# Where the weight pieces and the next pair's first chunks stand among the slots of a recurrent and feed-forward kernel

## The chip, the cores and the metric

The kernel runs on one core of one Trainium2 chip. The metric is device time in microseconds (us). Several runs are shown for a kernel and their median is what is compared; one further execution was taken by the hardware profiler, and every duration, wait and window in this document comes from that one.

## The reference

The input x holds 8 sequences of 512 tokens with 512 features. It is normalised, run through a bidirectional stack of four minimal gated recurrent layers, fused, added back, then run through a feed-forward layer with ternary weights and added back again. Cut to what matters:

```python
z = sigmoid(h @ Wz.T + bz)
h_tilde = tanh(h @ Wz.T + bz)            # the same weights serve z and h_tilde, and both directions
a = clip(1 - z, 1e-8, 1 - 1e-8)
h_new = linear_scan(a, z * h_tilde)      # along the tokens; backwards for the second direction
h = layernorm(h_new + (h if layer > 0 else 0))
...
x = x + concat(h_fwd, h_bwd) @ fusion_W.T + fusion_b
gamma = mean(abs(W)) + 1e-6              # for W_fc (2048 x 512) and W_proj (512 x 2048)
Wq = sign(W) * minimum(round(abs(W / gamma)), 1)
x = x + layernorm(gelu(layernorm(x) @ Wq_fc.T)) @ Wq_proj.T
```

The mean of all absolute values of a weight matrix must be known before any of its entries can be made ternary, and the ternary weights are needed only by the feed-forward part.

## The kernel before, in words

Everything runs on tiles of 128 partitions by 512 fp32 elements. A sequence has four feature **chunks** of 128 features (in the recurrent part, tokens along the free axis) and four token tiles (in the fusion and the normalisations). The work has two parts: a recurrent part over four **pairs** of sequences (the loop `for b in range(0, B, 2)` at L677), and a feed-forward part (L880 and below) that this change leaves alone.

**One chunk of a layer** is `gates` (L409): four matmuls into a PSUM tile u (L414), three activations on ScalarE that make a, t and z (`factors`, L428), then on VectorE a clip (L437), a product (L438), a scan (L442) and, in layers 1 and 2, the residual sum (L497). In the last layer the residual sums stand apart (`sums`, L503). A **state** is a sequence and a direction; a pair has four, and the order of a pair is layers 1, 2, 3, in each layer the four states, in each state the four chunks. Layer 0 has both directions in one chunk (`first_layer`, L444): four matmuls (L457), a scaling on VectorE (L464), the activations, clip, product and two scans, forwards and backwards. The eight layer-0 chunks of the next pair (`firsts`) are spread over the end of the present one.

**Normalising** a state turns its chunks into token tiles by transposes through the identity (`turned`, L293, into one of two PSUM tiles pt), takes statistics on VectorE (`stats`, L149 to L160, the power on GpSimd at L156), normalises on ScalarE (L166, L167) and turns the result back (`back`, transposes L302, activation L308). After the last layer only the statistics are taken (`norm_last`).

**Fusion** (`fusion`, L513) makes one token tile from eight matmuls over two PSUM tiles pu (L528), adds a bias (L523) and two scaled terms on VectorE (L536), and stores the tile to DRAM from SP's queue (L539). A pair has eight such tiles.

**The order is written out by hand**, per engine, as a sequence of **slots** (`slot`, L391). A slot issues, in this order: its own matmuls, the due scalings of layer-0 chunks, at most one or two shares of normalisation work for earlier states, the due clips and scans of layer-0 chunks, its own clip, product and scan (for fusion, the two scaled terms), the due residual sums, and the ScalarE ends of the shares. [...]

**The weight pieces** are a list `extra` that `slot` serves at its end (L401 to L406). There are 32 pieces of 128 by 512 for each of two passes. An `absolute` piece loads a part of a weight matrix from SP's queue (`staged`, L548, three buffers) and sums its absolute values on ScalarE (L557). `total` and `threshold` (L560, L565) then make the limits, with one small matmul that waits for a VectorE reduction. A `quantised` piece loads the part again, makes it ternary with two VectorE instructions (`ternary`, L171 and L172) and stores it to DRAM from SP's queue (L583, two buffers). Each time a piece is served, the loads of the next two are issued too. The list is filled with the 32 absolute pieces and the four small steps at the first pair, and with the 32 quantised pieces at the second (L679 to L690). The slot counter decides when one is served: every second slot in the first pair, every fourth from the second pair on (`pace`). So they fall in whatever the slot holds, layers or fusion alike.

**The next pair's layer-0 chunks:** two of the eight stand in the last state's last layer (before its chunks 1 and 3, the argument `between` of `layer`, L490), and one behind each of the first six fusion tiles (L722 to L726).

Of the kernel before, what the change touches and what calls it, by code (L numbers as in the profile page):

```python
# [24 lines left out]
def kernel(  # L25
# [28 lines left out]
    L = gru_wT.shape[0]  # L54
# [147 lines left out]
    NW = NQ * NC_  # L202
# [4 lines left out]
    with rec:  # L207
# [7 lines left out]
        now = [0]  # L215
# [20 lines left out]
        def shares(cap):  # L236


            last = []
            for q in (turns, backs):  # L240
                some = []
                for i in range(2):
                    if not q or not ready(q[0][0]):
                        break
                    at, piece = q[0][:2]
                    late = (at.at if isinstance(at, Tokens) else at) + piece < now[0]
                    if i >= cap and not late:
                        break
                    some.append(take(q))
                last = some + last  # L250
            return last
# [14 lines left out]
        def need(*keys):  # L266

            while any(left.get(k) for k in keys):
                slot(None, 2)
# [108 lines left out]
        def x_shares():  # L378
            return [take(q) for q in (xturns, xbacks) if q and ready(q[0][0])]

        pace = [2]
        extra = []

        stages = []
# [1 line left out]
        def due(kind):  # L386
            for s in [s for s in stages if s[0] <= now[0] and s[1] == kind]:
                stages.remove(s)
                s[2]()

        def slot(work=None, cap=1):  # L391
            end = work() if work is not None else None
            due("factors")
            last = shares(cap) + x_shares()
            due("scans")
            if end is not None:
                end()
            due("resid")
            for f in last:
                f()  # L400
            if extra and now[0] % pace[0] == 0:  # L401
                for piece in extra[:3]:
                    if piece[0] is not None:
                        piece[0]()
                        piece[0] = None
                extra.pop(0)[1]()  # L406
            now[0] += 1

        def gates(h, l, o, name, scans):  # L409

            def work():
                u = ps_u.tile([P, S], F32, tag="u", name=f"u_{name}")
                for c in range(NC_):
                    nc.tensor.matmul(  # L414
                        u, lhsT=gw[l][:, c, ts(o, P)], rhs=h[:, c, :],
                        start=(c == 0), stop=(c == NC_ - 1),
                    )
                z = zp.tile([P, S], F32, tag="z", name=f"z_{name}")
                zlive[0] += 1
                a, t = factors(u, z, l, o, name)  # L420

                def end():
                    product(a, z, t)
                    scans(a, z)
                return end
            return work
# [53 lines left out]
                return work  # L480
            return [chunk(o) for o in range(NC_)]

        def layer(s, l, between=()):
            while s not in state:
                slot(None, 2)
            need(s)
            zs = []
            h = state[s]
            for o in range(NC_):
                if between and o % 2:  # L490
                    slot(between.pop(0))

                def scans(a, z, o=o):
                    scan(z, a, z, s[1] == 1)
                    zs.append(z)
                    if l < L - 1:
                        nc.vector.tensor_tensor(z, z, h[:, o, :], ALU.add)  # L497
                    elif o == NC_ - 1:

                        for c in range(NC_):  # L500
                            def sums(c=c):
                                zlive[0] -= 1
                                nc.vector.tensor_tensor(h[:, c, :], zs[c], h[:, c, :], ALU.add)  # L503
                            stages.append((now[0] + c, "resid", sums))
                slot(gates(h, l, o, f"{s[0]}{s[1]}_{l}_{o}", scans))
            now[0] -= 1
            if l < L - 1:
                norm(s, zs, f"{s[0]}{s[1]}_{l}", 2)
            else:
                norm_last(s, f"{s[0]}{s[1]}_{l}")  # L510
            now[0] += 1
# [53 lines left out]
        def threshold(name, tot):  # L565

            pth = ps_u.tile([P, 512], F32, tag="u", name=f"pth_{name}")
            nc.tensor.matmul(pth[:, 0:1], lhsT=ones, rhs=tot, start=True, stop=True)
            absmean = const.tile([P, 1], F32, name=f"absmean_{name}")
            nc.vector.tensor_scalar(absmean, pth[:, 0:1], 1.0 / (H * F), Q_EPS, ALU.mult, ALU.add)  # L570
            hi = const.tile([P, 1], F32, name=f"hi_{name}")
            nc.vector.tensor_scalar(hi, absmean, 0.5, None, ALU.mult)
            lo = const.tile([P, 1], F32, name=f"lo_{name}")
            nc.vector.tensor_scalar(lo, absmean, -0.5, None, ALU.mult)
            limits[name] = (hi, lo)

        def quantised(part, i, name):
            w = []

            def go():  # L580
                q = qp.tile([P, 512], F32, tag="q", name=f"{name}q_{i}")
                ternary(q, w[0], limits[name])
                nc.sync.dma_start(out=wq[name][i // NC_][:, i % NC_, :], in_=q)  # L583
            extra.append([lambda: w.append(staged(part, i, f"{name}b")), go])

        def load_fc(i):
            fcq.append(wpool.tile([P, NC_, 512], F32R, tag=f"w{i}", name=f"fcq{i}"))
            nc.sync.dma_start(out=fcq[i].bitcast(F32), in_=wq["fc"][i])
# [74 lines left out]
        for i in range(2):  # L663
            s = const.tile([P, P], F32, name=f"fpick{i}")
# [11 lines left out]
            slot(lambda d=d: fold_sums(d), 2)  # L676
        for b in range(0, B, 2):  # L677
            last_pair = b + 2 == B
            if b == 2:  # L679
                pace[0] = 4  # L680
                for name, part in (("fc", fc_part), ("pw", proj_part)):
                    for i in range(NW):
                        quantised(part, i, name)
            if b == 0:
                for name, part in (("fc", fc_part), ("pw", proj_part)):
                    for i in range(NW):
                        absolute(part, i, name)
                    tots = []
                    extra.append([None, lambda n=name, tots=tots: tots.append(total(n))])
                    extra.append([None, lambda n=name, tots=tots: threshold(n, tots[0])])  # L690
            for l in range(1, L):
                if last_pair:
                    load_fc(l - 1)
                    if l == 1:
                        combined()
                        load_pw(0)
                for s in ((b, 0), (b, 1), (b + 1, 0), (b + 1, 1)):
                    if l == L - 1 and not last_pair and s[1] == 0:
                        norm_x(s[0] + 2, now[0])
                    if l == L - 1 and s[1] == 0:  # L700
                        load_pair("f", s[0])
                    if l == L - 2 and not last_pair and s[1] == 1:
                        load_pair("n", s[0] + 2)
                        load_xT(s[0] + 2)
                    if last_pair and s == (b, 1) and l == L - 2:
                        load_y(0)
                    if last_pair and s == (b, 0) and l == L - 1:
                        norm_y(0)
                    if l == L - 1 and not last_pair and s == (b + 1, 1):


                        firsts = first_layer(b + 2) + first_layer(b + 3)
                        layer(s, l, firsts)
                    else:
                        layer(s, l)
                    if s[0] == 1 and l == 1:
                        slot(lambda d=s[1]: fold(d))
                        if s[1] == 1:
                            slot(fold_bias)
            if last_pair:  # L720
                load_fc(L - 1)
            for i in range(2):  # L722
                for tile_ in fusion(b + i):
                    slot(tile_, 2)
                    if not last_pair and firsts:
                        slot(firsts.pop(0))  # L726
                if last_pair and i == 0:
                    load_pw(1)
                    load_pw(2)
# [18 lines left out]
    for i in range(2):  # L748
        s = const.tile([P, P], F32, name=f"pick{i}")
# [130 lines left out]
    for j in range(B * NF + LAG):  # L880
        b, k = divmod(j, NF)
# [74 lines left out]
```

## Time and profile before

| what | value |
|---|---|
| runs shown, median of 3 | 1767.56 us (1766.42 to 1767.70) |
| the profiled execution, its own time | 1769.31 us |
| its span, first to last instruction | 1767.3 us |
| what lies around the span | 2.0 us |
| mean granted TensorE clock | 0.990 |
| recurrent part in the span | 0 to 1268.3 us |
| feed-forward part | 1268.3 to 1767.3 us |

The recurrent part has stages that can be told apart in the trace by the first matmul of each: the layers by the groups of L414, the fusions by L528. From the start of one to the start of the next:

| pair | layer 1 | layer 2 | layer 3 | fusion, with the next pair's layer 0 |
|---|---|---|---|---|
| 0 | 61.6 to 152.2 | to 222.4 | to 297.7 | to 384.2 |
| 1 | 384.2 to 453.9 | to 523.5 | to 604.0 | to 691.7 |
| 2 | 691.7 to 762.1 | to 831.9 | to 914.4 | to 1002.1 |
| 3 | 1002.1 to 1072.6 | to 1141.5 | to 1208.4 | to 1268.3 (no layer 0) |

The absolute pieces run from 69.3 to 376.7 us, so through the whole first pair; the quantised ones from 436.3 to 1038.7 us, from the second pair's layer 1 into the last pair's layer 1. PE is TensorE's matmuls, PEld its weight loads, DVE is VectorE, ACT ScalarE, POOL GpSimd, SP the engine whose queue issues most DMAs. An fp32 matmul appears as two records.

### The profile page before, as it was taken

What the parts mean: (1) busy time and instruction counts of PE and PEld (TensorE: products, weight loads), DVE (VectorE), ACT (ScalarE), POOL (GpSimd) and SP (SyncE); (2) the same over time, 40 slices, a digit from 0 to 9 for tenths busy, and PEclk for the clock granted to TensorE, in tenths of its full rate; (3) what the DMA queues carried; (4) which work ended last, traced back from release to release, by engine and by line L of the source; (5) the groups of instructions that cost most, each with busy time, mean ns of one, the idle gap of its engine ahead of it and who ended that gap; (6) DMA issues with size and microseconds to landing.
All of it is one profiled execution on the core that took longest, in us unless ns stands there. A gap on an engine that the chain in (4) does not pass through costs nothing.

```text
span 1767.3 us, 19729 instructions
## 1 busy us (share of the span) xinstructions
PE 1721.4 (97%) x6424; PEld 1046.7 (59%) x6424; DVE 1451.1 (82%) x2865; ACT 1066.2 (60%) x1836; POOL 214.5 (12%) x334
## 2 busy tenths in 40 slices
PE   7989999999999999999999999999999999999998
PEld 3554554455554445555444455554588888888886
DVE  6977989779999977999897799997468778778876
ACT  2887884358886325787632588872156556566653
POOL 1111111111111111111111111111000000000000
PEclk9999999999999999999999999999999999999999
DMA  7002210110231111123101201101301101101100
GB/s 262 12 30 78 96 54 19 48 48 13 72 102 54 28 38 54 36 72 107 49 24 42 96 13 48 59 14 42 126 1 48 38 11 48 49 9 40 48 24 24
DMA packets 46454, 91.73 MB, mean 52 GB/s; under 512 B 5264, under 2 KB 5264, under 8 KB 45328
## 3 DMA queue, kind: packets, MB, share of 16 engines
q1 hardware_dynamic: 45488, 88.91, 14.8%
q10 hardware_dynamic: 864, 1.57, 0.3%
q8 instruction: 50, 0.82, 0.2%
q14 instruction: 52, 0.43, 0.1%
HBM read 65.30 MB, written 25.17 MB: 51 GB/s over the span
## 4 chain that ended last, share of the span: by engine, by line
PE 62%; DVE 29%; issue 6%; ACT 2%; POOL 0%; DVEq 0%; DMA 0%; POOLq 0%; ACTq 0%
PE u L414 16%; PE pu L528 12%; PE ph L782 12%; PE po L809 11%; DVE z L442 7%; DVE st L149 5%; DVE z L438 4%; PE u L457 4%; PE pt L293 3%; DVE z L497 2%; PE pf L302 2%; DVE a L437 2%; DVE mv L151 1%; DVE ve L155 1%; DVE st_x L149 1%
## 5 line engine op out<-in xcount | busy, mean ns | idle before, releaser
L414 PE MATMUL u<-xT,gw 128*128 128x512 f32 x768 | 351.1, 601 | 0.0
L414 PE MATMUL u<-h,gw 128*128 128x512 f32 x768 | 350.7, 600 | 0.0
L442 DVE TENSOR_TENSOR_SCAN z<-a,z 128x512 f32<-128x512 f32 x224 | 274.3, 1224 | 7.8
L149 DVE BATCH_NORM_STATS2 st<-pt 128x6 f32<-128x512 f32 x256 | 177.2, 692 | 71.7 <-PE pt L293 71.2
L786 ACT ACTIVATE g<-ph 128x512 f32<-128x512 f32 x128 | 76.4, 597 | 245.9 <-PE ph L782 245.9
L414 PEld LDWEIGHTS u<-xT,gw 128*128 128x128 f32 x768 | 141.2, 194 | 141.0 <-issue 141.0
L414 PEld LDWEIGHTS u<-h,gw 128*128 128x128 f32 x768 | 141.1, 194 | 140.7 <-issue 140.7
L156 POOL TENSOR_TENSOR rs<-ve,mhalf 128x1 f32<-128x1 f32 x192 | 122.9, 640 | 704.1 <-DVE nmu L160 649.1
L809 PE MATMUL po<-pwq,ghi 128*128 128x512 f32 x512 | 203.6, 398 | 0.0
L809 PE MATMUL po<-pwq,glo 128*128 128x512 f32 x512 | 199.9, 390 | 0.0
L782 PE MATMUL ph<-yhi,fcq 128*128 128x512 f32 x512 | 199.8, 390 | 0.0
L782 PE MATMUL ph<-ylo,fcq 128*128 128x512 f32 x512 | 199.7, 390 | 0.0
L431 ACT ACTIVATE a<-u,ngb 128x512 f32<-128x512 f32 x192 | 131.2, 683 | 99.6 <-PE u L414 98.7
L438 DVE TENSOR_TENSOR z<-z,t 128x512 f32<-128x512 f32 x224 | 153.7, 686 | 16.6 <-ACT z L433 16.6
L167 ACT ACTIVATE tok<-pt,nmr,rs 128x512 f32<-128x512 f32 x192 | 149.2, 777 | 6.4
L797 DVE TENSOR_TENSOR acc<-acc,g 128x512 f32<-128x512 f32 x112 | 77.4, 691 | 91.1 <-ACT g L786 90.1
L433 ACT ACTIVATE z<-u,gb 128x512 f32<-128x512 f32 x192 | 132.6, 691 | 0.0
L431 ACT ACTIVATE a<-z,ngb 128x512 f32<-128x512 f32 x32 | 23.1, 722 | 179.7 <-DVE z L464 179.7
L432 ACT ACTIVATE t<-u,gb 128x512 f32<-128x512 f32 x192 | 131.0, 682 | 0.0
L302 PE MATMUL pf<-ident,tok 128*128 128x128 f32 x768 | 116.8, 276 | 13.0 <-ACT tok L167 10.4
L293 PEld LDWEIGHTS pt<-ident,z 128*128 128x128 f32 x640 | 78.8, 142 | 84.6 <-issue 52.4
L166 ACT ACTIVATE nmr<-nmu,rs 128x1 f32<-128x1 f32 x192 | 56.5, 294 | 107.5 <-POOL rs L156 96.8
(138 smaller groups left out, 2711.0 us busy)
## 6 DMA issues: line engine op xcount, KB each, us to landing
xn<-in_x_dram SPq DMA_DIRECT2D x32, 256.0 KB, 4.6
xf<-in_x_dram SPq DMA_DIRECT2D x32, 256.0 KB, 4.3
x<-xf SPq DMA_DIRECT2D x32, 256.0 KB, 2.0
xy<-x SPq DMA_DIRECT2D x32, 256.0 KB, 4.1
out_dram<-xy SPq DMA_DIRECT2D x32, 256.0 KB, 2.0
xT<-in_xt_dram SPq DMA_DIRECT2D x7, 1024.0 KB, 7.0
fca<-in_fc_wT_dram SPq DMA_DIRECT2D x16, 256.0 KB, 2.9
pwa<-in_proj_wT_dram SPq DMA_DIRECT2D x16, 256.0 KB, 2.7
```

The costliest lines, as they stand in the source:

```text
L149: nc.vector.bn_stats(st, src)
L167: nc.scalar.activation(dst, src, AF.Identity, bias=nmr, scale=rs)
L293: nc.tensor.transpose(pt[:, ts(c, P)], zs[c][:, ts(t, P)], ident)
L302: nc.tensor.transpose(pf[:, ts(t, P)], toks[t][:, ts(c, P)], ident)
L414: nc.tensor.matmul(u, lhsT=gw[l][:, c, ts(o, P)], rhs=h[:, c, :], start=(c == 0), stop=(c == NC_ - 1),)
L431: nc.scalar.activation(a, u, AF.Sigmoid, bias=ngb[:, l, o : o + 1], scale=-1.0)
L433: nc.scalar.activation(z, u, AF.Sigmoid, bias=gb[:, l, o : o + 1])
L438: nc.vector.tensor_tensor(z, z, t, ALU.mult)
L442: nc.vector.tensor_tensor_scan(dst[:, d], a[:, d], z[:, d], 0.0, ALU.mult, ALU.add)
L528: nc.tensor.matmul(pu, lhsT=hs[d][:, c, ts(t, P)], rhs=fw[:, d * NC_ + c, :], start=(c == 0), stop=(c == NC_ - 1),)
L782: nc.tensor.matmul(ph, lhsT=w, rhs=ys[b][c][i], start=(c == 0 and i == 0), stop=(c == NC_ - 1 and i == 1),)
L809: nc.tensor.matmul(po[b][t], lhsT=part[:, ts(t, P)], rhs=pwq[k // NP_][:, k % NP_, :], start=(k == 0 and i == 0), stop=(k == NF - 1 and i ...
```

## The change

The pace is gone: a slot no longer serves pieces. A new function `pieces(n)` serves n of them where it is called, and it is called in two places.

In the first pair, inside `layer`: behind every second chunk of layers 1 and 2 and behind every chunk of layer 3, as long as more than 32 entries are left in the list. With 36 entries ahead of the quantised ones and 8, 8 and 16 places, 32 are served there; the last four (two absolute pieces, the second total and threshold) go to the first fusion.

Behind every fusion tile of every pair, one piece behind tiles 0 and 2 of a sequence and two behind tiles 1 and 3. The quantised pieces are put on the list from the start, so eight of them are served in the first pair's fusion and twelve in each of the next two; none is left for the layers.

The two layer-0 chunks leave the last layer. All eight stand behind fusion tiles: two each behind tiles 0 and 2 of the first sequence, one each behind its tiles 1 and 3 and behind tiles 0 and 1 of the second.

```diff
-        pace = [2]
         extra = []
...
+        def pieces(n):
+
+            for _ in range(min(n, len(extra))):
+                for piece in extra[:3]:
+                    if piece[0] is not None:
+                        piece[0]()
+                        piece[0] = None
+                extra.pop(0)[1]()
...
         def slot(work=None, cap=1):
...
-            if extra and now[0] % pace[0] == 0:
-                for piece in extra[:3]:
-                    if piece[0] is not None:
-                        piece[0]()
-                        piece[0] = None
-                extra.pop(0)[1]()
             now[0] += 1
...
-        def layer(s, l, between=()):
+        def layer(s, l):
...
             for o in range(NC_):
-                if between and o % 2:
-                    slot(between.pop(0))
...
                 slot(gates(h, l, o, f"{s[0]}{s[1]}_{l}_{o}", scans))
+
+                if s[0] < 2 and (l == L - 1 or o % 2) and len(extra) > 2 * NW:
+                    pieces(1)
...
-            if b == 2:
-                pace[0] = 4
-                for name, part in (("fc", fc_part), ("pw", proj_part)):
-                    for i in range(NW):
-                        quantised(part, i, name)
             if b == 0:
...
+                for name, part in (("fc", fc_part), ("pw", proj_part)):
+                    for i in range(NW):
+                        quantised(part, i, name)
...
-                    if l == L - 1 and not last_pair and s == (b + 1, 1):
-
-
-                        firsts = first_layer(b + 2) + first_layer(b + 3)
-                        layer(s, l, firsts)
-                    else:
-                        layer(s, l)
+                    layer(s, l)
...
+            firsts = [] if last_pair else first_layer(b + 2) + first_layer(b + 3)
             for i in range(2):
-                for tile_ in fusion(b + i):
+                for t, tile_ in enumerate(fusion(b + i)):
                     slot(tile_, 2)
-                    if not last_pair and firsts:
-                        slot(firsts.pop(0))
+                    pieces(1 + t % 2)
+                    for _ in range(2 if i == 0 and t % 2 == 0 else 1):
+                        if firsts:
+                            slot(firsts.pop(0))
```

## The prediction, on record before the changed kernel was run

> **What bounds the kernel now.** First the page as a whole: TensorE (PE) is busy nearly throughout and most of the final chain is PE's, but a modelled busy share hides short stalls, and almost a third of the chain is VectorE's (DVE).
>
> ```profile
> PE 1721.4 (97%) x6424; PEld 1046.7 (59%) x6424; DVE 1451.1 (82%) x2865; ACT 1066.2 (60%) x1836; POOL 214.5 (12%) x334
> ...
> PE 62%; DVE 29%; issue 6%; ACT 2%; POOL 0%; DVEq 0%; DMA 0%; POOLq 0%; ACTq 0%
> ```
>
> So I read it by stage, in the view of windows (columns: stretch, length, then busy us and instructions of PE, PEld, DVE, ACT, POOL, then clock and DMA): layer 3 and fusion of pair 1, layer 3 of pair 2, layers 2 and 3 of pair 3, and the few us after a stall.
>
> ```profile
> 523.50:604.00 80.50, 75.18 (x251) 38.53 (x250) 74.56 (x151) 44.61 (x75) 13.69 (x22) 0.98 0.17 56
> 604.00:691.70 87.70, 86.65 (x274) 43.30 (x273) 67.58 (x129) 28.07 (x47) 10.41 (x16) 1.00 0.15 45
> 831.90:914.40 82.50, 77.11 (x251) 39.03 (x250) 74.86 (x152) 44.75 (x76) 13.75 (x22) 0.96 0.17 55
> 1072.60:1141.50 68.90, 68.90 (x258) 37.54 (x257) 63.08 (x129) 56.31 (x98) 10.80 (x16) 1.00 0.09 31
> 1141.50:1208.40 66.90, 66.54 (x234) 34.95 (x233) 61.62 (x126) 47.48 (x83) 10.86 (x17) 1.00 0.13 48
> 598.60:605.00 6.40, 6.40 (x16) 3.08 (x16) 6.05 (x13) 1.57 (x3) 1.13 (x2) 0.77 0.13 45
> ```
>
> What PE needs is counted from starts in the timeline: eight 512-column records take 3.43 us (583.78 to 587.21, 0.429 each), four transposes 0.44.
>
> ```profile
> 551.32 0.33 PE L302 MATMUL pf<-ident,tok 128*128 128x128 f32 x1 [2.40 <-ACT tok L167]
> ...
> 583.78 3.60 PE L414 MATMUL u<-h,gw 128*128 128x512 f32 x8
> ...
> 587.21 0.60 PE L293 MATMUL pt<-ident,h 128*128 128x128 f32 x4
> ...
> 587.65 3.60 PE L414 MATMUL u<-h,gw 128*128 128x512 f32 x8
> ...
> 598.37 0.48 PE L293 MATMUL pt<-ident,xT 128*128 128x128 f32 x1 [2.93 <-DVE xT L503]
> ```
>
> Pair 1's layer 3: 144 large records (18 chunks) and 107 transposes, 61.8 + 11.7 = 73.4 us needed of 80.5, so 7.1 lost; pair 2's 9.1. Pair 3's layer 3, without layer-0 chunks and without pieces, needs 54.9 + 11.6 = 66.5 of 66.9. Pair 1's fusion: 176 and 98, 75.5 + 10.7 = 86.2 of 87.7. So the loss sits in layer 3 of pairs 1 and 2, where DVE is busy 93% (74.56 of 80.5) and the chain of waits over the window is DVE's.
>
> Where in it? Two stalls, both above: a back transpose waits 2.40 us for ScalarE's tok, and a transpose 2.93 us for a residual sum. Pair 2 has both, at 860 and 909. Both are DVE's lateness: from the end of a chunk's matmuls to the end of its scan takes 3.9 us at best; in pair 1's layer 3 it starts at 6.2, falls to 3.9 with the first stall, and climbs to 11.5 before the second. In pair 0's same slots, with layer-0 chunks but no ternary work, it reaches 9.1 (one stall of 1.65 at 293.6); in pair 3's it never passes 5.3.
>
> [...] after the 2.93 us stall the clock was 0.77 over 6.4 us, about 1.5 us lost on top; the stall of 2.40 was followed by no dip. [...] DVE's rows in the timeline keep program order. So a ternary piece delays all that stands behind it on DVE, and a late statistic delays PE. [...]
>
> **The change, part by part.** Prices, from the groups by form:
>
> ```profile
> L172 DVE SCALAR_TENSOR_TENSOR fcq<-fcb,hi_fc,fcq 128x512 f32<-128x512 f32 x16 | 12.0, 751 | 0.6
> L171 DVE TENSOR_SCALAR fcq<-fcb,lo_fc 128x512 f32<-128x512 f32 x16 | 7.7, 478 | 0.0
> L557 ACT ACTIVATE fca<-fca 128x512 f32<-128x512 f32 x16 | 10.0, 624 | 0.0
> ```
>
> A quantised piece is 0.48 + 0.75 = 1.23 us of DVE, an absolute one 0.62 + 0.20 (its accumulator read) = 0.82 of ACT. A layer-0 chunk is 3.43 us of PE and on DVE 0.68 (L464) + 0.42 (L437) + 0.69 (L438) + 2 × 1.22 (L442) = 4.23.
>
> *Layer 3, pairs 1 and 2.* Out go two layer-0 chunks (6.9 PE, 8.5 DVE) and about five pieces (6.2 DVE). What stays is pair 3's layer 3 in all but the other sequence statistics: 67.0, half a us above PE's need. Pair 1: 80.5 - 6.9 (moved, not saved) - 67.0 = 6.6 saved; pair 2: 82.5 - 6.9 - 67.0 = 8.6. The second stall also loses its place: these transposes move from the slot before the last chunk to the first fusion slot, two large slots (3.9 + 6.9 us) behind the sum they need; with a lateness of about 8 they find it done.
>
> *Layer 3, pair 0.* The chunks go (75.3 - 6.9 = 68.4) and with them the 1.65 us stall, but an absolute piece stands in every slot: in slots 2 to 4 ACT carries 3 × 0.68 of gates, 1.07 of tok, 0.79 of back and 0.82, 4.7 against PE's 4.3. That is 1.2 us of lateness; afterwards ACT has room. The first threshold's matmul comes one slot, not two, behind its reduction: it may wait 0 to 2 us. I take 67.6: 0.8 saved.
>
> *Layers 1 and 2.* Pairs 1 and 2 lose six and seven pieces in them (7.4 and 8.6 us of DVE), but PE is within 0.5 to 1.3 us of its 69.1. I take 70.2 and 69.2 for each pair: -0.7 together. Pair 0 keeps its absolute pieces at about the old rate: no change, bounds -3 to +3, since its stalls (layer 1 stands 14 us above need) depend on small shifts.
>
> *Fusion.* PE gains 6.9 us: 86.2 + 6.9 = 93.1. DVE, not covered by pieces in before, gets 8.5 for the chunks and eight more pieces (12 for 4), 9.8: 67.6 + 18.3 = 85.9 in about 96 us, 89%. Pair 3's layer 2 runs at 92% with no stall, so the sum fits; the question is the order. I laid DVE's queue against PE slot by slot, entering fusion some 4 us late. Through the six early chunks both advance alike (by the third fusion tile PE 34, DVE 35), so the lateness stays. The tight place is the first half's end: tile 3 with two pieces, chunk 6, then tile 4, whose transposes need a pt buffer that is freed by a tok behind those statistics. There I get a PE wait of about 2 us, where before had 0.68 and 0.33 (at 669 and 670). Then DVE recovers; two pieces behind the last tile push the next layer 1 about 1 us late (in the 70.2). PSUM's four u buffers come free in time throughout. I take 1.5 more idle than before for pairs 1 and 2 and 1.0 for pair 0, whose first tiles carry almost no ternary work. Bounds: 1.5 less (no wait at all) to 6 more (a wait past 2.4 with the clock's 1.5, and one at layer 1).
>
> *Queues.* Two loads and a store of 256 KB per piece move to fusion on SP's queue. Loads run two pieces ahead, at least one tile (7 us), and land in 2.7 to 3.7 us; a store waits for its ternary piece, and behind it stand the next tile's store, read by nobody before the last pair, and later loads with tiles to spare. DMA is 15% busy there. Cost nothing; if a load were late, DVE would stop for up to 3.7 us. GpSimd's work is the same.
>
> Sum on the span: -6.6 - 8.6 - 0.8 - 0.7 + 1.5 + 1.5 + 1.0 = -12.7, so 1754.6; with the 2.0 around it the profiled execution would be 1756.6. It lay 1.75 above the median; -12.7 on the median 1767.56 gives 1755.
>
> **Rivals.**
> - *Clean*: fusion swallows everything; its idle (1.5, 1.5 and 0.3 us) falls instead of growing. 1767.6 - 16.7 = 1751 at no growth, 1748 at none left. For it: 89% is less than layer 2's 92%. Against: fusion's DVE work comes in lumps of 3.6 and 2.5 us.
> - *Bound moved*: each fusion loses 3 to 5 us more than before, one wait with the clock's dip: -16.7 + 9 to 15, so 1760 to 1766. For it: twelve pieces share the slots that get the two chunks.
> - *Slower*: two waits past 2.4 us in every fusion (pt buffers at tile 4 and again at the start of layer 1), each 2.9 + 1.5 = 4.4 with the dip. Three pairs at 8.8 are 26.4 against 16.7 saved in layers 1 to 3: about 1777. It decides from 16.7 / 3 = 5.6 us more idle per fusion. Against: layers 1 and 2 at equal load show single waits of 0.3 to 0.8.
> - *The layer-3 stalls stay*, being the layer's own and not the load's: 1767. Pair 3 speaks against it.
>
> **How the numbers follow.** A measurement of this kernel tells about 0.2% (3.5 us) from no change. Forecast (1751 to 1759) 0.58, clean 0.12, bound moved 0.18 (0.13 of it beyond 0.2%), stalls stay 0.05, slower 0.07. Faster 0.58 + 0.12 + 0.13 = 0.83, same 0.10 (0.05 of the moved bound and the 0.05), slower 0.07. The range 1749 to 1764.5 leaves out the clean case's low end (0.04), the moved bound's last part (0.04) and the last two cases (0.12), 0.2 in all.
>
> **What would show it.** Layer 3 of pairs 1 and 2 near 67 us without waits on L503 or tok above 1 us; lateness of scans there below about 8.5; fusion near 96 with its largest PE wait at the pt transposes of tile 4; no clock dip after 170 us. Wrong if fusion takes over 100 us, or if pair 0's first three layers shift by more than 3.

## The result, and the profile after

Six runs of each kernel: 1757.47 us after (1756.77 to 1759.76) against 1768.08 before. The ratio is 0.9943, with a 95% interval from 0.9932 to 0.9953: 0.57% faster, 10.6 us on the medians. The prediction had 12.7 us, 1755 on the median of its day. The profiled execution took 1756.91 us, its span 1754.9; predicted were 1756.6 and 1754.6. That these two agree to 0.3 us is partly luck, as the stages show.

The page of the changed kernel, its lines of engines and of the chain by engine: TensorE carries 82% of the final chain where it had 62%, VectorE 10% where it had 29%.

```profile
PE 1713.5 (98%) x6424; PEld 1043.4 (59%) x6424; DVE 1456.2 (83%) x2865; ACT 1068.7 (61%) x1836; POOL 214.7 (12%) x334
...
PE 82%; DVE 10%; issue 4%; ACT 2%; POOL 1%; DMA 0%; DVEq 0%; POOLq 0%
```

The windows of the changed kernel (stretch, length, busy us and instructions of PE, PEld, DVE, ACT, POOL, clock, DMA share, GB/s): pair 0's fusion, layer 3 and fusion of pair 1, the same of pair 2, and the last pair's layer 1.

```profile
285.00:383.80 98.80, 94.80 (x300) 47.27 (x299) 79.88 (x154) 32.65 (x56) 12.14 (x18) 1.00 0.18 58
523.10:588.80 65.70, 65.70 (x227) 34.07 (x226) 59.29 (x124) 42.77 (x72) 12.10 (x20) 1.00 0.06 16
588.80:686.60 97.80, 95.81 (x299) 47.69 (x298) 84.00 (x159) 30.74 (x50) 12.14 (x18) 0.98 0.24 73
825.80:891.50 65.70, 65.70 (x227) 34.11 (x226) 59.29 (x124) 42.81 (x73) 12.17 (x20) 1.00 0.06 17
891.50:988.00 96.50, 94.35 (x299) 47.08 (x298) 84.04 (x159) 30.75 (x50) 12.14 (x18) 1.00 0.22 74
988.00:1060.40 72.40, 69.43 (x258) 37.40 (x257) 66.83 (x141) 56.77 (x99) 11.37 (x18) 1.00 0.12 41
```

Layer 3 of pairs 1 and 2 is now busy to the last tenth on PE. Fusion is not: 192 large records at 0.429 us and 104 transposes at 0.109 need 93.7. All stages side by side:

| stage | before | predicted | after |
|---|---|---|---|
| pair 0, up to layer 3 | 222.4 | 222.4 | 218.9 |
| pair 0, layer 3 | 75.3 | 67.6 | 66.1 |
| pair 0, fusion | 86.5 | 94.4 | 98.8 |
| pair 1, layers 1 and 2 | 139.3 | 139.4 | 139.3 |
| pair 1, layer 3 | 80.5 | 67.0 | 65.7 |
| pair 1, fusion | 87.7 | 96.1 | 97.8 |
| pair 2, layers 1 and 2 | 140.2 | 139.4 | 139.2 |
| pair 2, layer 3 | 82.5 | 67.0 | 65.7 |
| pair 2, fusion | 87.7 | 96.1 | 96.5 |
| pair 3, layer 1 | 70.5 | 70.5 | 72.4 |
| pair 3, from layer 2 to the end of fusion | 195.7 | 195.7 | 195.5 |
| feed-forward part | 499.0 | 499.0 | 499.0 |

The timeline shows what the fusion waits for (PE's rows of the changed kernel; the bracket has the idle time before the row and what ended it; tok is a normalised token tile, written by ScalarE). In order: pair 0, a layer-0 chunk behind the scaled terms of a fusion tile; pair 1, the transposes behind fusion tile 4; pair 3's layer 1, transposes behind its first chunks.

```profile
325.03 3.70 PE L459 MATMUL u<-xT,gw 128*128 128x512 f32 x8 [1.84 <-DVE xf L538]
...
651.10 0.66 PE L293 MATMUL pt<-ident,z 128*128 128x128 f32 x4 [1.99 <-ACT tok L167]
...
998.27 0.66 PE L293 MATMUL pt<-ident,z 128*128 128x128 f32 x4 [2.38 <-ACT tok L167]
```

The second stands in all three fusions (349.6, 651.1, 953.8), each time with about 2.0 us.

### The profile page after: what moved, and what is told of

Same layout as the page of the kernel before. It is cut to its first block, busy times and chain, and to the rows that moved or that the text cites. A ratio compares the mean times of both kernels' runs of the same rounds, so it can differ in the third digit from the quotient of the medians.

```text
span 1754.9 us, 19733 instructions
## 1 busy us (share of the span) xinstructions
PE 1713.5 (98%) x6424; PEld 1043.4 (59%) x6424; DVE 1456.2 (83%) x2865; ACT 1068.7 (61%) x1836; POOL 214.7 (12%) x334
## 4 chain that ended last, share of the span: by engine, by line
PE 82%; DVE 10%; issue 4%; ACT 2%; POOL 1%; DMA 0%; DVEq 0%; POOLq 0%
PE u L416 33%; PE ph L781 12%; PE po L808 11%; PE pu L530 11%; PE pt L293 5%; PE u L459 4%; PE pf L302 4%; DVE st L149 2%; DVE z L444 2%; DVE z L440 1%; PE py L192 1%; DVE zf L444 1%; DVE mv L151 1%; ACT tok L167 1%; DVE z L496 1%
## 5 line engine op out<-in xcount | busy, mean ns | idle before, releaser
L416 PE MATMUL u<-xT,gw 128*128 128x512 f32 x768 | 348.8, 597 | 0.0
L416 PE MATMUL u<-h,gw 128*128 128x512 f32 x768 | 346.5, 594 | 0.0
L459 PE MATMUL u<-xT,gw 128*128 128x512 f32 x256 | 117.3, 605 | 2.2 <-DVE xf L538 1.8
```

The costliest lines, as they stand in the source:

```text
L416: nc.tensor.matmul(u, lhsT=gw[l][:, c, ts(o, P)], rhs=h[:, c, :], start=(c == 0), stop=(c == NC_ - 1),)
L459: nc.tensor.matmul(u, lhsT=gw[0][:, c, ts(o, P)], rhs=xT[b][:, c, :], start=(c == 0), stop=(c == NC_ - 1),)
```

## The experiments

Eight kernels were timed beside the kernel before. The question after the result: which of the two parts brought the gain, and what does fusion wait for? My theory was that layer 3 loses by VectorE's lateness and that either part alone would cure most of it; the rival was that the parts add up and the chunks carry most.

**1. The pieces alone.** The new `pieces` calls, with the layer-0 chunks in their old places:

```diff
+        def layer(s, l, between=()):
+                if between and o % 2:
+                    slot(between.pop(0))
...
-                    for _ in range(2 if i == 0 and t % 2 == 0 else 1):
-                        if firsts:
-                            slot(firsts.pop(0))
+                    if not last_pair and firsts:
+                        slot(firsts.pop(0))
```

> Only the weight pieces are placed anew; two layer-0 chunks stay in the last layer. Theory (layer 3 loses because VectorE is late there, and either part alone brings most of the lateness below the point where TensorE stalls): layer 3 of pairs 1 and 2 about 75 us with one wait of about 1.7 on the residual sum, as pair 0 had before, no wait on tok; fusion about 89 to 90; about 11 us under before, so as fast as the whole change or nearly. Rival (the two parts add up, the chunks carry most): at most 4 us under before.

Measured: 1766.47 us, ratio 0.9992 (0.9984 to 1.0000). Layer 3 of pair 1, pair 1's fusion, layer 3 and fusion of pair 2, and pair 3's layer 1, with pair 0's fusion ahead of them, and the transpose that waits in layer 3:

```profile
294.80:387.80 93.00, 88.67 (x277) 44.42 (x276) 70.68 (x139) 30.37 (x53) 10.47 (x16) 0.98 0.19 60
527.00:602.70 75.70, 73.71 (x251) 37.91 (x250) 68.53 (x140) 44.67 (x76) 13.72 (x22) 1.00 0.05 15
602.70:692.20 89.50, 86.94 (x275) 43.29 (x274) 74.92 (x143) 28.58 (x47) 10.43 (x16) 1.00 0.26 80
831.40:907.00 75.60, 73.65 (x250) 37.87 (x249) 68.57 (x140) 44.60 (x76) 13.74 (x22) 1.00 0.04 15
907.00:997.80 90.80, 88.25 (x275) 44.03 (x274) 74.97 (x143) 28.60 (x47) 10.47 (x16) 0.98 0.24 79
997.80:1070.20 72.40, 69.43 (x259) 37.40 (x257) 66.82 (x141) 56.84 (x99) 11.35 (x18) 1.00 0.12 41
```

```profile
598.64 0.33 PE L293 MATMUL pt<-ident,xT 128*128 128x128 f32 x1 [1.66 <-DVE xT L505]
```

The theory had layer 3 nearly right (75.7 and 75.6 for about 75, one wait of 1.7 on the residual sum, none above 0.4 on tok): 4.8 and 6.9 us saved. It had the sum wrong. Pair 0's fusion is 6.5 us longer than before, pairs 1 and 2 by 1.8 and 3.1, pair 3's layer 1 by 1.9: what layer 3 gains, fusion and the last layer 1 give back. The theory that either part alone brings the gain falls.

**2. The chunks alone.** The kernel before, with its pace, and all eight chunks behind fusion tiles as in the change.

```diff
-                if between and o % 2:
-                    slot(between.pop(0))
...
+            firsts = [] if last_pair else first_layer(b + 2) + first_layer(b + 3)
...
-                    if not last_pair and firsts:
-                        slot(firsts.pop(0))
+                    for _ in range(2 if i == 0 and t % 2 == 0 else 1):
+                        if firsts:
+                            slot(firsts.pop(0))
```

> Only the layer-0 chunks move behind the fusion tiles; the pieces keep their pace of one in 2 or 4 slots. Theory: the wait on the residual sum goes, the 2.4 us wait on tok in layer 3 of pairs 1 and 2 stays, since pieces and sequence statistics still fall together there: layer 3 about 69 to 71, fusion about 95, about 8 us under before. With the first experiment the two gains sum to far more than the whole change gave (about 19 for 10). Rival (additive): what the first experiment lacks to 10, so 6 to 10, with both waits gone.

Measured: 1753.32 us, ratio 0.9917 (0.9904 to 0.9931): 14.9 us under before, and 4 us faster than the whole change. Its windows (pair 0's fusion, layer 3 and fusion of pair 1, the same of pair 2) and the wait in layer 3:

```profile
284.90:379.00 94.10, 94.06 (x299) 47.22 (x298) 72.69 (x139) 35.71 (x66) 12.17 (x18) 1.00 0.11 37
518.10:587.70 69.60, 67.20 (x226) 35.01 (x225) 62.58 (x131) 42.51 (x73) 12.13 (x20) 0.98 0.19 61
587.70:682.70 95.00, 94.36 (x298) 47.02 (x297) 79.51 (x150) 30.87 (x50) 12.38 (x18) 1.00 0.14 45
822.50:890.70 68.20, 65.74 (x226) 33.98 (x225) 62.71 (x131) 42.45 (x73) 12.20 (x20) 1.00 0.21 62
890.70:985.70 95.00, 94.36 (x298) 47.01 (x297) 79.60 (x150) 30.87 (x50) 12.38 (x18) 1.00 0.13 45
```

```profile
546.00 0.48 PE L302 MATMUL pf<-ident,tok 128*128 128x128 f32 x1 [2.40 <-ACT tok L167]
```

The stages are as expected: the wait on tok stays, layer 3 stands at 69.6 and 68.2. Fusion with single ternary pieces, five of which run in it, takes 95.0; pair 0's, which has none, 94.1. The sum is not: about 8 us were expected, and 14.9 came. So against the chunks alone, the new places of the pieces save 3.9 and 2.5 us in layer 3 and cost 4.7, 2.8 and 1.5 in the fusions and 1.9 in the last layer 1. The rival is nearer: the chunks carry all of the gain. But the parts don't add up to it either (1.7 and 14.9 for 10.6), since one of them is a loss beside the other.

**3. No piece behind tile 3.**

```diff
-                    pieces(1 + t % 2)
+                    pieces((2, 2, 1, 0, 1, 2, 3, 1)[4 * i + t])
```

> The whole change, but the twelve pieces of a fusion stand 2, 2, 1, 0 behind the tiles of the first sequence and 1, 2, 3, 1 behind those of the second, so none behind tile 3. Theory: the two ternary pieces (2.4 us of VectorE) ahead of the statistics that tile 4's transposes wait for make the 2.16 us wait there: it falls below 0.5 in all three fusions, and the wait at the start of the last pair's layer 1 shrinks from 2.5 to about 1; about 6 us under the whole change, 17 under before. Rival (the wait comes from the two chunks doubled behind tile 2): it stays within 0.5 of 2.16, and the time within 1 us of the whole change.

Measured: 1760.74 us, ratio 0.9961 (0.9949 to 0.9974), slower than the whole change. Pair 0's fusion, and fusion and next layer 1 of pairs 1 and 2; then the matmul of the second threshold, and a transpose at the start of pair 2's layer 1:

```profile
283.80:386.10 102.30, 97.48 (x301) 48.36 (x299) 78.65 (x150) 32.60 (x56) 12.17 (x18) 0.97 0.17 54
592.90:687.90 95.00, 94.36 (x299) 47.07 (x298) 82.71 (x155) 30.77 (x50) 12.16 (x18) 1.00 0.24 72
687.90:759.70 71.80, 69.71 (x259) 37.38 (x258) 66.14 (x140) 56.99 (x99) 11.39 (x18) 1.00 0.27 97
894.30:989.30 95.00, 94.36 (x299) 47.07 (x298) 82.90 (x155) 30.77 (x50) 12.16 (x18) 1.00 0.23 73
989.30:1063.70 74.40, 71.00 (x258) 37.97 (x257) 68.06 (x143) 57.10 (x99) 11.39 (x18) 0.98 0.13 42
```

```profile
310.50 0.59 PE L570 MATMUL pth_pw<-tot_pw,ones 128*128 128x1 f32 x2 [4.18 <-DVE tot_pw L564]
...
692.49 0.66 PE L293 MATMUL pt<-ident,zf 128*128 128x128 f32 x4 [1.00 <-ACT tok L167]
```

The point in question is answered: fusion of pairs 1 and 2 falls to 95.0, and the wait at tile 4 (1.99 in the trace of the whole change, the expectation's 2.16) to 0.60, about what it was before (0.68). The time is worse for two reasons that I had not foreseen. My pattern put the second total and its threshold behind one tile, and the threshold's matmul then waits 4.18 us for a reduction at the end of VectorE's queue, with a clock of 0.97 over that fusion. And four pieces behind the last two tiles make the next layer 1 late: 71.8 and 74.4 us where the whole change had 70.3 and 72.4. Part of the lateness only moves on.

**4. Another PSUM buffer for the threshold.**

```diff
-            pth = ps_u.tile([P, 512], F32, tag="u", name=f"pth_{name}")
+            pool, tag = (ps_f, "pf") if name == "pw" else (ps_u, "u")
+            pth = pool.tile([P, 512], F32, tag=tag, name=f"pth_{name}")
```

> The whole change, but the second threshold's small matmul takes its PSUM tile from the transposes' pool and not from the four u tiles. Theory: the 1.84 us wait of a layer-0 chunk on the scaled terms of a fusion tile in pair 0 comes from the turn of the u tiles that the threshold takes; it goes, and pair 0's fusion is about 2 us shorter (96.9), unless the wait at tile 4 takes it up. Rival (VectorE is late there anyway): the wait shows at the next chunk or tile, fusion stays at about 98.9.

Measured: 1756.09 us, ratio 0.9933 (0.9920 to 0.9947). The layer-0 chunk now follows its forerunner without a wait:

```profile
317.76 3.68 PE L459 MATMUL u<-xT,gw 128*128 128x512 f32 x8
...
321.71 3.60 PE L459 MATMUL u<-xT,gw 128*128 128x512 f32 x8
325.15 3.60 PE L530 MATMUL pu<-fw,xT 128*128 128x512 f32 x8
```

So the 1.84 us were the turn of the u tiles. Pair 0's fusion came to 98.1 and not to 96.9, with a mean clock of 0.98 in that window (1.00 in the whole change): by an estimate from these two (0.02 of 98.1 us) some 2 us, enough for the missing 1.2. The time is 1.4 us under the whole change, with overlapping intervals.

**5. Chunks moved, old pace, the last layer bare.** The second kernel with one condition more.

```diff
-            if extra and now[0] % pace[0] == 0:
+            if extra and now[0] % pace[0] == 0 and not hold[0]:
...
             for l in range(1, L):
+                hold[0] = b > 0 and l == L - 1
...
+            hold[0] = False
```

> The layer-0 chunks move as in the change; the pieces keep the old pace, but no quantised piece stands in a last layer (its turns fall to later layers 1 and 2 and, at the end, to the last pair's fusion). Theory (what the change should have done: the pieces hurt in the last layer, where sequence statistics come on top, and in fusion in lumps, not in layers 1 and 2 or in fusion one by one): layer 3 of pairs 1 and 2 at 65.7 as in the whole change, layers 1 and 2 at 69.5 to 70, fusion at 95, so 6 us under chunks only: about 1747, 1.2% under before. Rival (each piece costs its time wherever it stands, since VectorE is full everywhere): no better than chunks only, about 1753.

Measured: 1751.55 us, ratio 0.9908 (0.9891 to 0.9924): 1.8 us under the chunks alone, with overlapping intervals, where 6 were expected. Layer 3 fell to 66.9 and 67.4, not to 65.7; the last pair's layers 2 and 3, which got pieces, rose by 1.2 and 1.1. The wait on tok in pair 1's layer 3 is halved, not gone:

```profile
545.28 0.33 PE L302 MATMUL pf<-ident,tok 128*128 128x128 f32 x1 [1.17 <-ACT tok L167]
```

The lateness with which layer 3 begins is layer 2's: at one piece in four slots it swings between 4.0 and 5.4 through layer 2, ends there at 5.4 and starts layer 3 at 6.2, where the whole change, with bare slots, has 3.9 and 5.0. The last piece of layer 2 runs on VectorE at 518.7, and the wait on tok ends at 545.3, six chunks on. So a piece costs by what stands behind it, here some six slots on.

**6. The whole change without the ternary instructions.** The kernel leaves out the ternary step, so its weights stay as they were loaded.

```diff
-    stgp = rec.enter_context(tc.tile_pool(name="stg", bufs=3))
+    stgp = rec.enter_context(tc.tile_pool(name="stg", bufs=5))
...
-                q = qp.tile([P, 512], F32, tag="q", name=f"{name}q_{i}")
-                ternary(q, w[0], limits[name])
-                nc.sync.dma_start(out=wq[name][i // NC_][:, i % NC_, :], in_=q)
+                nc.sync.dma_start(out=wq[name][i // NC_][:, i % NC_, :], in_=w[0])
```

> The whole change without the two ternary instructions: a quantised piece loads its part and stores it as it is (five load buffers in place of three, none for the result), so the loads and stores of the pieces stay and VectorE's 1.23 us of each goes. Theory (VectorE's queue is what the pieces cost in fusion): fusion of pairs 1 and 2 falls from 97.8 and 96.5 to about 94.5, the last pair's layer 1 from 72.4 to 70.5, about 6 us under the whole change. Rival (it is SP's queue or the DMA traffic): the waits stay, time within 1.5 of the whole change.

Measured: 1746.07 us, ratio 0.9876 (0.9862 to 0.9891), 11.4 us under the whole change. Fusion of pairs 1 and 2 and the last pair's layer 1:

```profile
585.50:679.50 94.00, 93.96 (x298) 47.15 (x297) 72.53 (x138) 30.70 (x50) 12.14 (x18) 1.00 0.24 76
883.80:977.90 94.10, 94.06 (x299) 47.23 (x298) 72.63 (x140) 30.81 (x50) 12.15 (x18) 1.00 0.23 76
977.90:1047.90 70.00, 69.40 (x258) 37.40 (x257) 64.47 (x137) 56.74 (x99) 11.38 (x18) 1.00 0.12 42
```

The same loads and stores run (76 GB/s in fusion, 73 and 74 in the whole change), and the waits at tile 4 are gone in all three fusions. It is VectorE's queue, not SP's and not the transfers. In this run the stores no longer wait for VectorE either and there are five load buffers, so alone it would not part the two queues; but in the changed kernel's three fusions VectorE never waits for a load, all its waits there are for PE and ScalarE. In pair 0 the 1.84 us of the u tiles stay (96.4). Of the 39 us that the 32 pieces take on VectorE (32 × 1.23), 11 show in the time of the whole change. I had put it at 6.

**7. Tile 3 bare from the second pair on.**

```diff
-                    pieces(1 + t % 2)
+                    pieces(1 + t % 2 if b == 0 else (2, 2, 1, 0, 2, 2, 2, 1)[4 * i + t])
```

> The whole change; pair 0 as it is, from pair 1 on the pieces stand 2, 2, 1, 0 and 2, 2, 2, 1 behind the tiles, so that no reduction is followed at once by the matmul that waits for it and only one piece stands behind the last tile. Theory: fusion of pairs 1 and 2 at 95.0, the next layer 1 no later than in the whole change (70.3 and at most 72.4): about 4 us under the whole change, so 1753. Rival (the lateness only moves on, as it did in the third experiment, and comes back at the start of the next layer 1): within 1 us of the whole change.

Measured: 1752.83 us, ratio 0.9916 (0.9901 to 0.9930), 4.6 us under the whole change: the time is as expected, the path to it only half. Fusion took 96.2 and not 95.0: VectorE runs the two pieces behind tile 4 from 656.0 to 658.4, and the statistics behind them make the transposes behind tile 5 late; layer 1 got better than expected with one piece behind the last tile (69.4 and 71.3).

```profile
588.40:684.60 96.20, 94.37 (x299) 47.12 (x298) 85.14 (x161) 30.77 (x50) 12.15 (x18) 1.00 0.26 79
684.60:754.00 69.40, 69.17 (x259) 37.55 (x258) 63.72 (x135) 56.92 (x99) 11.38 (x18) 1.00 0.26 88
```

```profile
662.84 0.66 PE L293 MATMUL pt<-ident,z 128*128 128x128 f32 x4 [1.79 <-ACT tok L167]
```

**8. Pieces by lateness.** Chunks moved, the first pair's pieces at the old pace, and the quantised pieces by hand where scans are on time and no transposes that need a statistic come soon after.

```diff
...
+            if pace[0] and extra and now[0] % pace[0] == 0:
+                pieces(1)
...
+                k = 8 * (s[0] % 2) + 4 * s[1] + o
+                if s[0] >= 2 and k in {1: (8, 11, 14), 2: (1, 4, 7)}.get(l, ()):
+                    pieces(1)
...
                     slot(tile_, 2)
+                    if b >= 2:
+                        pieces((2, 2, 1, 0, 1, 2, 2, 0)[4 * i + t])
```

> The layer-0 chunks move as in the change; the first pair keeps its absolute pieces at every second slot; the quantised pieces stand where the other runs show VectorE's scans on time: three each in layers 1 (chunks 9, 12, 15 of 16) and 2 (chunks 2, 5, 8), and ten in a fusion as 2, 2, 1, 0 and 1, 2, 2, 0, none in a last layer, none behind tile 3 or the last tile. Theory (a piece costs nothing where lateness has room to fall before the next transpose that needs it): fusions 94 to 95, layer 3 at 65.7, layers 1 and 2 at 69.0 to 70; about 1746, as good as the run without ternary work and 1.2% under before. Rival (32 pieces always cost some 6 us somewhere): 1751 to 1753, like the best so far.

Measured: 1747.56 us, ratio 0.9886 (0.9869 to 0.9902): 20.8 us under before, twice the gain of the change, and the best kernel that does all the work. Layer 3 and fusion of pair 1, layers 2 and 3 and fusion of pair 2:

```profile
519.60:585.60 66.00, 65.68 (x227) 34.06 (x226) 59.24 (x124) 42.75 (x72) 12.12 (x20) 1.00 0.06 16
585.60:680.60 95.00, 94.36 (x299) 47.07 (x298) 84.02 (x159) 30.75 (x50) 12.15 (x18) 1.00 0.24 75
750.50:821.20 70.70, 69.53 (x258) 37.45 (x257) 66.89 (x138) 55.92 (x98) 10.80 (x16) 1.00 0.30 101
821.20:886.90 65.70, 65.70 (x226) 34.09 (x225) 59.28 (x124) 42.78 (x73) 12.16 (x20) 1.00 0.06 17
886.90:981.90 95.00, 94.36 (x298) 47.08 (x297) 84.00 (x159) 30.75 (x50) 12.14 (x18) 1.00 0.23 72
```

VectorE does the same work in these two fusions as in the whole change's: busy 84.0 us, with ten ternary pieces inside the window, in both kernels (the whole change's last two fall past its end). The whole change took 2.8 us more, of which an estimated 1.3, the difference between its two fusions, by the clock of 0.50 from 651.63 to 655.04, and 1.5. Inside the windows it is the same load in another order. Over the whole run it is not: this kernel issues ten pieces per fusion and not twelve, puts the other twelve into layers 1 and 2, and has none of them in pair 0's fusion, which takes 94.0 where the whole change took 98.8.

## Why the prediction was right, and where not

*What bounds the kernel* was read rightly: the loss sat in layer 3, by VectorE's lateness. The measure that carried it, the end of a chunk's scan less the end of its matmuls, over the sixteen chunks of pair 1's layer 3 (us, worked out from the trace):

```
before        6.2 6.3 6.4 7.7 7.3 6.4 3.9 4.0 5.0 5.7 6.7 9.0 9.0 10.4 11.5 7.4
pieces alone  5.0 5.1 5.5 5.6 5.2 4.3 3.9 3.9 4.9 5.6 6.6 7.7 7.7 9.1 9.1 8.2
chunks alone  6.2 6.3 6.4 7.7 7.3 6.4 3.9 4.0 5.0 5.7 6.7 9.0 9.0 9.0 8.5 9.7
after         5.0 5.1 5.2 5.3 4.9 4.0 3.9 3.9 4.9 5.6 6.6 7.7 7.7 7.7 7.2 7.2
```

Against the kernel before, the pieces alone lower columns 1 to 6 and 12 to 15, the chunks alone columns 14 and 15 (the two chunks stood before chunks 14 and 16). After stays below the predicted 8.5.

*Layer 3, pairs 1 and 2*: predicted 67.0, measured 65.7. The transposes of statistics that moved into fusion (227 records of PE where 234 were assumed) and the half us of idle time that I added account for it. Both waits went, and with them half-clock time: the kernel before has three half-clock stretches of 3.41 us in these two layers (from 598.2, 861.0 and 908.8), each of which, at a clock of 0.50, costs an estimated 1.7 us, the changed kernel none. That the second wait goes because its transposes move behind two large slots, and not because VectorE is relieved, is what the runs of the parts show: with the pieces alone 1.66 us of it stay at a lateness of 9.1, with the chunks alone none at 8.5 to 9.7.

*Pair 0's layer 3*: 66.1 for 67.6; here too eight transposes (0.9 us) moved on into fusion. The absolute piece in every slot cost at most 0.4 us (with the old pace, in run 2, the stage took 65.6).

*Fusion* is the term that was mis-sized. I took 1.5, 1.5 and 1.0 us more idle time than before in pairs 1, 2 and 0; measured, with the 6.9 us of the chunks taken off, the stages are 3.2, 1.9 and 5.4 longer. Of each, 0.9 is PE's own work: the eight transposes that leave layer 3 (104 there before, 96 after) and that the sum did not add to fusion. The other 2.3, 1.0 and 4.5 are time above PE's need. The mechanism and its place were named: the transposes behind tile 4, a pt buffer freed by a tok behind two ternary pieces, about 2 us, and it is 1.99: in pair 1 VectorE runs the two pieces from 644.71 to 647.16 and the statistics behind them from 647.67, and the transposes start at 651.10. Three more things were missing. The sentence that the four u buffers come free in time throughout overlooked that the second threshold takes one of them in pair 0 and so shifts the turn: 1.84 us, gone in run 4. I gave pair 0 less of the tile-4 wait for its lighter first tiles, but the wait hangs on the two pieces just ahead and was there in full (2.00). And after one of the three waits the clock was 0.50 for 3.41 us (below).

*Two pieces behind the last tile*: counted at 1 us per pair in layer 1, and measured so in pairs 1 and 2 (70.3 for 70.2); in pair 3, where four instructions of `combined` (L603 and L604, 2.1 us) stand right behind them on VectorE, the wait was 2.38 and the stage 1.9 longer. I had left that at zero.

*Pair 0 up to layer 3* was predicted unchanged and came out 3.5 us shorter, past the 3 us that the prediction named as a sign of being wrong. It is not the change: the chunks-only kernel has the old code in these stages and reaches layer 3 at 219.3, the best kernel at 220.2. The kernel before's profiled execution had more half-clock time there: mean clock 0.94 and 0.84 in its 61.6 to 152.2 and 152.2 to 170.0, against 0.96 and 0.91 in the like stretches after: five half-clock stretches of 3.41 us against three, which at a clock of 0.50 makes an estimated 3.4 us. So of the 12.4 us between the two spans about 9 are the change's, which agrees with the 10.6 between the medians and their interval (8 to 12 us).

*Queues*: free, as said; run 6 and VectorE's waits in the fusions show it. (A piece moves one load and one store to fusion, not two loads.)

*The rivals*: the three fusions have 7.8 us of new time above need, where the forecast said 4 and the moved bound 9 to 15. In that term the rival was nearer. That the profiled execution still lands within 0.3 us of the forecast is a sum of misses: the fusions took 6.5 us more than forecast and pair 3's layer 1 1.9; layer 3 took 4.1 less and pair 0's start, by the half-clock stretches, 3.5 less. That is luck. None of the other rivals' signs is there. Of the forecast's own signs one failed: there is a clock dip after 170 us, at 651.6.

*Readings that were slightly off.* A window also counts instructions that straddle its edges, so layer 3 has 104 transposes and not 107, and pair 1's fusion 96 and not 98. The wait of 2.40 without a dip was one of two: pair 2's, 2.47 before 859.9, was followed by half clock from 861.0.

What the prediction did not ask is what the parts do alone. It priced layer 3 as one package. Taken apart, the chunks bring 14.9 us and the new places of the pieces, beside them, lose about 4. In pairs 1 and 2 a part of that is order: run 7 has the same twelve pieces per fusion in another order, and fusion and the next layer 1 together are 2.5 us (an estimated 1.3 of it the half-clock stretch, as in the last run) and 1.4 us shorter than in the whole change. The last run gains 3.2 and 3.7 there, but with ten pieces per fusion; how much of the rest is order and how much amount is not shown. In pair 0's fusion, where the whole change places eight ternary pieces and the second threshold and the last run neither, 4.8 us come back by taking work out. That the whole change is faster says nothing about one of its two halves.

What stays open: the waits of pair 0's layers 1 and 2 (about 14 us above PE's need in the changed kernel, by an estimate some 5 of it from three stretches of 3.41 us at a clock of 0.50) were left alone, and the best kernel still loses 1.1 and 1.8 us in layer 2 of pairs 1 and 2, where pieces stand three slots apart and the lateness climbs to 5.9 and 6.5; that they stand too close was not tried out.

## What to carry to other kernels

Where a program is ordered by hand, whether an engine has room at a place is not told by its busy share there (pair 3's layer 2 at 92% ran without waits, pair 1's fusion at 86% lost 4 us) but by how late it is at the next point where another engine needs a buffer back: tabulate that lateness slot by slot and put movable work where it is at its floor and has slots enough to fall again (some six here, as far as run 5 tells). Don't put two pieces just ahead of such a point: two behind tile 3 cost 2 us in each fusion, while twos elsewhere, as in the last run, left fusion at the 95.0 that single pieces gave. A change of two parts is worth two runs: here one part was a gain of 15 us that hid a loss of 4.

## What the runs showed of the hardware that was not expected

In these traces the length of a wait alone does not tell whether a half-clock stretch follows it. In the changed kernel the wait at tile 4 is the same 1.99 us in pairs 1 and 2, with the same work around it; after the first the clock was 0.50 for 3.41 us, after the second 1.00, and the stages differ by 1.3 us, 97.8 and 96.5. The window that holds the wait (for the second, its larger part) and the one behind it, for both:

```profile
648.22:651.63 3.41, 1.42 (x11) 0.89 (x10) 2.15 (x9) 3.00 (x6) 1.47 (x2) 1.00 0.65 211
651.63:655.04 3.41, 3.41 (x7) 1.32 (x6) 3.07 (x7) 1.85 (x3) 0.66 (x1) 0.50 0.00 1
...
952.01:955.42 3.41, 1.59 (x7) 1.07 (x8) 2.09 (x7) 2.75 (x5) 1.18 (x2) 1.00 0.32 120
955.42:958.84 3.42, 3.42 (x16) 1.98 (x15) 3.24 (x7) 1.07 (x2) 0.66 (x1) 1.00 0.00 0
```

In the traces of the kernel before and of the changed one, each half-clock stretch between 30 and 1700 us lasts 3.41 us (6.83 from 151.03 in the kernel before, twice that), and within a trace they start whole multiples of 3.413 us apart: in the kernel before at 598.18, 861.00 and 908.79, which is 77 and 14 multiples. Laid out in steps of that length, the first wait falls wholly into one, from 648.22, of which PE is idle for 1.99 us. The second is cut by the border at 952.01 into 0.17 and 1.83, the wait of 2.38 that ends at 998.27 by the one at 996.38 into 0.49 and 1.89, and the 2.40 of the kernel before, at 551, into 1.47 and 0.93; none of these three was followed by half clock. Between 200 and 1250 us, four steps at full clock in these two traces had 1.99 us or more of idle PE (1.99 after; 2.32, 2.73 and 2.92 before), and half clock followed each of them; it followed none with 1.89 or less. Earlier in the program it also followed steps with 1.89 (from 57.71 after) and 1.82 (from 58.87 before). PE's ends are modelled, so these idle times are estimates from the two traces.

The prediction's bound of 2.4 us, taken from one pair of waits, does not hold: half clock followed the wait of 1.99 us in pair 1's fusion, and not the ones of 2.38 and 2.40. What makes the clock fall is not shown; the traces show only what stood ahead of it.
